# Seven half-size products for the scores of two tiles, and gathered rows added up on TensorE

## The chip, the cores and the metric

The kernel runs on one core of a Trainium2 chip. The metric is device time in microseconds (us); the time before is the median of three runs, 2519.51 us (2517.99 to 2520.62). Everything is fp32. A core has five engines with queues of their own[...]: PE (TensorE, matrix products, results in PSUM), DVE (VectorE), ACT (ScalarE), POOL (GpSimd, which here issues the gathers) and SP (which issues the other DMAs). PSUM is used here as three "pairs" of 2 x 512 columns and two single banks, `pv` and `pt`.

## The reference, cut to what matters

Four layers are added to an image batch x of 4 x 512 x 32 x 32; layers 0 to 2 are two attentions and a gate and are left as they are. Layer 3 reads a memory of 2048 rows of 512 numbers:

```python
q = jnp.transpose(x, (0, 2, 3, 1)).reshape(-1, C)      # 4096 tokens x 512, group-normalised
att = q @ mempool.T                                    # 4096 x 2048 scores
vals, idx = jax.lax.top_k(att, k)                      # k = 8
vals = jax.nn.softmax(vals, axis=1)
att_sparse = jnp.zeros_like(att).at[rows, idx].set(vals)
out = att_sparse @ mempool                             # 8 weighted rows per token
```

The result, turned back to channels first, is added to layer 3's input.

## The kernel before, in words

Layers 0 to 2 fill the first 2012 us or so; their matrix products already use seven half-size products in places (`seven`, L1048 for the sums). Layer 3 is the end. The memory, transposed, lies in SBUF as four tiles `memT[k]` of 128 channels x 2048 items (`load_memory`). Each image has 1024 tokens, 8 tiles of 128 (`tiles`, 32 in all). Per tile:

- `attention` (L1521): for each half of the items, 2 blocks of 512 items x 4 blocks of channels, so 16 matmuls of 128x128 by 128x512 per tile, 8 into each pair of banks; ScalarE copies each half to `att` (L1526).
- `pick`: VectorE's MAX8 (L1541) and FIND_INDEX8 (L1543) over 2048 scores; eight indirect DMAs on POOL (L1546) gather the eight rows to `got`; `tmx` (L1552) and the Exp on ScalarE (L1555) make the weights `et` and their sum `rs`; SP loads the tile's layer input `xr`.
- `read`: `weigh` (L1563, L1564) divides the weights by the sum; VectorE makes acc, the first row times its weight (L1591), and adds the other seven (L1593); four transposes on TensorE (L1598) turn acc back to channels first.
- `put`: VectorE adds `xr` (L1603) and SP stores the result (L1604).

The loop runs these on different tiles: at step s, scores of tile s, search of tile s-1, put of s-3, read of s-2. The order on each engine is written out by hand: an instruction passed through `pin` stays in the order of the code with the other pinned ones of its engine. The last two tiles (`read_last`, L1579) are read by another way: eight diagonal matrices of the weights (`diagonals`, L1570), and 32 matmuls that add up and turn back the eight rows in PSUM. `prepare3` loads and normalises the next image's tokens in four ScalarE steps (L1506). The first tile's scores are made ahead of the last projection of layer 2 (`put_out2`, L199, L1478), and that projection's results are layer 3's input for the fourth image.

Of the kernel before, what the change touches and what calls it, by code (L numbers as in the profile page):

```python
# [41 lines left out]
def fast_net(ctx: ExitStack, tc: tile.TileContext, a: dict, out: bass.AP, flag: bass.AP):  # L42
# [13 lines left out]
    def pin(ins):  # L56

        return tc.keep_in_program_order(ins)
# [131 lines left out]
    def tokens(src):  # L190
        return lambda k, n: src[:, k, n * NB:(n + 1) * NB]

    def project(w, rhs, m, at, evacuate, name="proj"):


        ps = place(at, f"{name}_{m}")
        for n in range(T // NB):
            for k in range(KC):
                pin(nc.tensor.matmul(  # L199
                    ps[:, n, :], w[:, k, m * P:(m + 1) * P], rhs(k, n),  # L200
                    start=(k == 0), stop=(k == KC - 1),
                ))
        evacuate(flat2(ps))
# [1259 lines left out]
        nc.vector.tensor_mul(  # L1463
            I["o"][:, m, n * NB:(n + 1) * NB], I.pop(("pv", m, n)), I.pop(("rb", m, n)))

    def put_out2(b):
        I = img[b]
        s1 = l2[b][1]
        mv = small.tile([P, KC, 2], F32, tag="mv", name=f"mv_d{b}")

        def add_out(m, ps):
            st = small.tile([P, 2, 6], F32, tag="bnst", name=f"st_d{b}_{m}")
            for n in range(T // NB):
                xr = apool.tile([P, NB], F32, tag="xr", bufs=2, name=f"xr_c{b}_{m}_{n}")
                nc.sync.dma_start(out=xr, in_=x1[b][:, m, n * NB:(n + 1) * NB])
                pin(nc.scalar.activation(
                    xr, xr, AF.Identity, bias=I["tb"][:, m:m + 1], scale=s1[:, m:m + 1]))
                nc.vector.tensor_add(xr, ps[:, n * NB:(n + 1) * NB], xr)  # L1478
                nc.sync.dma_start(out=x2[b][:, m, n * NB:(n + 1) * NB], in_=xr)
                nc.vector.bn_stats(st[:, n, :], xr)  # L1480
            nc.vector.bn_aggr(mv[:, m, :], st.rearrange("p i s -> p (i s)"))

        for m in range(KC):
            project(I["Wp"], tokens(I["o"]), m, None, lambda ps: add_out(m, ps), f"p2_{b}")
        gc3 = const.tile([P, 2, KC], F32, tag=f"gc3_{b}", name=f"gc3_{b}")
        l3[b] = (mv, gc3)

# [21 lines left out]
            ))  # L1509
            yield  # L1510

    def attention(b, tt, between=None):

        nm = f"{b}_{tt}"
        att = eight_k([P, NI], f"att_{nm}")
        for i, (lo, hi) in enumerate(
                ((0, T), (T, T + NB), (T + NB, NI)) if (b, tt) == tiles[-1] else ((0, T), (T, NI))):
            sc = flat2(next_pair())
            for i0 in range(lo, hi, NB):
                for k in range(KC):  # L1520
                    pin(nc.tensor.matmul(  # L1521
                        sc[:, i0 - lo:i0 - lo + NB],
                        xn3[b][:, k, tt * P:(tt + 1) * P], memT[k][:, i0:i0 + NB],
                        start=(k == 0), stop=(k == KC - 1),
                    ))
            pin(nc.scalar.copy(att[:, lo:hi], sc[:, 0:hi - lo]))  # L1526
            if between is not None and i == 0:
                between()
        return att

    def pick(b, tt, att):

        nm = f"{b}_{tt}"
        top = small.tile([P, TOPK], F32, tag="top", name=f"top_{nm}")
        if (b, tt) == tiles[-1]:
            tops = small.tile([P, 3, TOPK], F32, tag="tops", bufs=1, name="tops")
            for i, (lo, hi) in enumerate(((0, T), (T, T + NB), (T + NB, NI))):
                pin(nc.vector.max(tops[:, i, :], att[:, lo:hi]))
            pin(nc.vector.max(top, tops.rearrange("p i n -> p (i n)")))
        else:  # L1540
            pin(nc.vector.max(top, att))  # L1541
        ix = small.tile([P, TOPK], mybir.dt.uint32, tag="ix", name=f"ix_{nm}")
        pin(nc.vector.max_index(ix, top, att))  # L1543
        got = big("qkv"[(b * TC + tt) % 3], f"got_{nm}").rearrange("p k (i c) -> p (k i) c", c=C)
        for i in range(TOPK):
            pin(nc.gpsimd.indirect_dma_start(  # L1546
                out=got[:, i, :], out_offset=None, in_=a["mem"],
                in_offset=bass.IndirectOffsetOnAxis(ap=ix[:, i:i + 1], axis=0),
                bounds_check=NI - 1, oob_is_err=False,
            ))  # L1550
        nmx = small.tile([P, 1], F32, tag="nmx", name=f"tmx_{nm}")
        pin(nc.vector.tensor_scalar_mul(nmx, top[:, 0:1], -1.0))  # L1552
        et = small.tile([P, TOPK], F32, tag="et", name=f"et_{nm}")
        rs = small.tile([P, 1], F32, tag="rs", name=f"trs_{nm}")
        nc.scalar.activation(et, top, AF.Exp, bias=nmx, scale=1.0, accum_out=rs)  # L1555
        i = (b * TC + tt) % 3
        xr = eT_flat[:, i * NB:(i + 1) * NB].rearrange("p (k q) -> p k q", q=P)
        nc.sync.dma_start(out=xr, in_=x2[b][:, :, tt * P:(tt + 1) * P])
        return got, et, rs, xr

# [9 lines left out]
            pin(nc.scalar.activation(dg[:, i, :], ident, AF.Identity, scale=et[:, i:i + 1]))  # L1570
        return dg

    def read_last(b, tt, picked, dg):

        got, et, rs, xr = picked
        tp = next_bank().rearrange("p (k q) -> p k q", q=P)
        for i in range(TOPK):
            for m in range(KC):
                pin(nc.tensor.matmul(  # L1579
                    tp[:, m, :], got[:, i, m * P:(m + 1) * P], dg[:, i, :],  # L1580
                    start=(i == 0 and m == 0), stop=(i == TOPK - 1),
                    skip_group_check=True,
                ))
        return tp, xr

    def read(b, tt, picked):
        got, et, rs, xr = picked
        nm = f"{b}_{tt}"
        weigh(et, rs, nm)
        acc = apool.tile([P, NB], F32, tag="rb", bufs=2, name=f"acc_{nm}")  # L1590
        pin(nc.vector.tensor_scalar_mul(acc, got[:, 0, :], et[:, 0:1]))  # L1591
        for i in range(1, TOPK):
            pin(nc.vector.scalar_tensor_tensor(  # L1593
                acc, got[:, i, :], et[:, i:i + 1], acc, ALU.mult, ALU.add
            ))
        tp = next_bank().rearrange("p (k q) -> p k q", q=P)
        for m in range(KC):
            pin(nc.tensor.transpose(tp[:, m, :], acc[:, m * P:(m + 1) * P], ident))  # L1598
        return tp, xr

    def put(b, tt, done):
        tp, xr = done
        pin(nc.vector.tensor_add(xr, tp, xr))  # L1603
        nc.sync.dma_start(out=out_v[b, :, :, tt * P:(tt + 1) * P], in_=xr)  # L1604
# [244 lines left out]
        places7[key] = nine[3 * i:3 * i + 3]  # L1849
    places7["Wq"] = places7["Wp"]  # L1850
    nc.gpsimd.tensor_scalar_mul(same, same, 8.0 / T)
    tiles = [(b, tt) for b in range(B) for tt in range(TC)]
    atts, picks, sums = {}, {}, {}
    scores2(0, UNITS2[0])
    for b in range(B):
# [29 lines left out]
            first7[2]()  # L1885
        apply2(b, UNITS2[-1])
        if last:
            atts[0] = attention(*tiles[0], lambda: invert2(b))
            finish2(b)
            put_out2(b)  # L1890
            continue
        over_keys(b, *UNITS2[-1][:2])
        at_border[0] = True
# [39 lines left out]
    ahead, behind = iter(()), chain(behind, norm3(B - 1))  # L1933
    end = len(tiles)
    diags = {}

    def pick_last(s):
        at = s - 1
        picks[at] = pick(*tiles[at], atts.pop(at))
        put(*tiles[s - 3], sums.pop(s - 3))  # L1940
        weigh(*picks[at][1:3], f"{tiles[at][0]}_{tiles[at][1]}")

    for s in range(end + 3):
        closing = end - 1 <= s <= end
        if closing:
            pick_last(s)
        if s < end:
            b, tt = tiles[s]
            if s > 0:
                atts[s] = attention(b, tt, (lambda: diags.update(  # L1950
                    {0: diagonals(0, picks[end - 2][1])})) if closing else None)
        if 0 <= s - 1 < end and not closing:
            picks[s - 1] = pick(*tiles[s - 1], atts.pop(s - 1))
        if s == end:
            diags[1] = diagonals(1, picks[end - 1][1])
        if s >= 3 and not closing:
            put(*tiles[s - 3], sums.pop(s - 3))
        if 0 <= s - 2 < end:
            at = s - 2
            sums[at] = (read(*tiles[at], picks.pop(at)) if at < end - 2  # L1960
                        else read_last(*tiles[at], picks.pop(at), diags[at - end + 2]))
        if s < end and tt == 2:
            ahead = prepare3(b + 1) if b + 1 < B else iter(())
        if s < end and tt >= 2:
            next(ahead, None)
        if s < end and 1 <= s <= TC:
            next(behind, None)
        if s == TC + 2:
            check_range()
        if s == TC + 4:  # L1970
            again = nc.values_load(flag, min_val=0, max_val=1)
    return again


# [702 lines left out]
```

## Time and profile before

| | |
|---|---|
| median of three runs | 2519.51 us |
| the profiled execution | 2519.18 us, span 2517.5 us, mean granted TensorE clock 0.998 |
| busy, share of the span | PE 98%, DVE 72%, ACT 41%, POOL 49% |
| layer 3, from the second tile to the last score (2068.2 to 2493.5, 425.3 us) | PE 425.3, DVE 345.8, ACT 89.2, POOL 270.0 us busy |
| chain that ended last, share of the span | PE 87%, of which L1521 17%; DMA 4%; DVE 3%; ACT 2% |

Busy time of PE is modelled, so it is read together with the idle time and the chain. The chain of waits is followed back from the last instruction: where it stays on one engine that engine sets the pace. In a group, the number after the count is the busy total and then the mean of one; after the last bar stands the engine's idle time ahead of the group and what ended it. PE records are shown singly: a matmul here leaves two, a transpose one.

### The profile page before, as it was taken

The page shows a single profiled execution, that of the slowest core. Times are in us where ns is not written, and L with a number is a line of the kernel's source. Part 1 is how long each engine was busy: PE and PEld are TensorE (multiplying, and loading weights), DVE is VectorE, ACT ScalarE, POOL GpSimd, SP SyncE. Part 2 cuts the span into 40 slices and gives each one's busy share as a digit, 9 for nine tenths or more (in the row PEclk, how much of TensorE's full clock was granted, in tenths as well). Part 3 has the DMA queues.
Part 4 walks back from the last instruction along what each step waited for, and adds up shares of the span by engine and source line. Part 5 has one row for each costly group of instructions (what it writes and reads, how often), then busy time and mean ns, then how long its engine had stood idle before and what let it go on. Part 6 is the DMA issues. An engine that isn't in the chain of part 4 may idle for free.

```text
span 2517.5 us, 48084 instructions
## 1 busy us (share of the span) xinstructions
PE 2474.3 (98%) x18512; PEld 1174.9 (47%) x18512; DVE 1822.0 (72%) x2962; ACT 1022.8 (41%) x1245; POOL 1224.0 (49%) x1688
## 2 busy tenths in 40 slices
PE   9999999999999999999999999999999999999998
PEld 4344534555355534555633633453363344444445
DVE  5789568875788548886768677676757647887876
ACT  1567346652666336651253145225324512121212
POOL 3266526553465426554274247127405617566665
PEclk9999999999999999999999999999999999999999
DMA  2597448872698538893301230131114046667666
GB/s 85 156 233 218 118 128 228 239 218 84 176 241 233 137 89 218 241 244 122 109 25 52 108 130 18 63 110 46 55 46 138 24 138 189 214 190 220 182 189 178
DMA packets 190033, 367.20 MB, mean 146 GB/s; under 512 B 32986, under 2 KB 96474, under 8 KB 185571
## 3 DMA queue, kind: packets, MB, share of 16 engines
q1 hardware_dynamic: 109712, 186.58, 23.9%
q0 software_dynamic: 49152, 142.79, 20.6%
q10 hardware_dynamic: 30930, 34.66, 5.1%
q8 instruction: 149, 2.44, 0.4%
q14 instruction: 90, 0.73, 0.1%
HBM read 190.10 MB, written 39.58 MB: 91 GB/s over the span
## 4 chain that ended last, share of the span: by engine, by line
PE 87%; DMA 4%; DVE 3%; ACT 2%; issue 1%; POOL 1%; SPq 0%; ACTq 0%; POOLq 0%
PE pair L1521 17%; PE pair L1121 12%; PE pair L1369 8%; PE pv L578 8%; PE pair L513 6%; PE pair L199 6%; PE pair L539 6%; PE pt L471 5%; PE pt L1406 4%; PE pv L1406 4%; PE pair L1247 4%; PE pt L767 4%; DMA s<-ss 3%; ACT e L546 2%; DVE out L1048 1%
## 5 line engine op out<-in xcount | busy, mean ns | idle before, releaser
L528 POOL DMA_DIRECT2D s<-ss x512 | 258.1, 511 | 398.6 <-issue 115.0
L552 DVE STREAM_TRANSPOSE eT<-e 128x1024 f32<-128x1024 f32 x256 | 316.6, 1237 | 186.5 <-ACT e L546 186.1
L1546 POOL DMA_INDIRECT got<-in_mem,ix x256 | 279.3, 1091 | 213.2 <-DVE tmx L1552 144.4
L1363 ACT ACTIVATE eT<-pair 128x1024 f32<-128x1024 f32 x256 | 248.5, 1022 | 314.8 <-PE pair L1369 188.8
L567 DVE BATCH_NORM_STATS2 st<-e 128x6 f32<-128x256 f32 x1024 | 350.7, 404 | 0.0
L1387 POOL TENSOR_TENSOR e<-eT 128x1024 f32<-128x1024 f32 x96 | 239.0, 2493 | 171.7 <-ACT eT L1363 122.6
L546 ACT ACTIVATE e<-pair 128x1024 f32<-128x1024 f32 x256 | 250.4, 1022 | 165.8 <-PE pair L539 137.2
L519 ACT COPY ss<-pair 128x1024 f32<-128x1024 f32 x256 | 247.2, 1020 | 86.7 <-PE pair L513 42.7
L513 PE MATMUL pair<-k,q 64*32 64x512 f32 x4096 | 267.3, 598 | 12.7 <-ACT e L546 12.7
L578 PEld LDWEIGHTS pv<-eT,v 128*64 128x64 f32 x4096 | 221.1, 137 | 72.0 <-issue 55.2
L578 PE MATMUL pv<-eT,v 128*64 128x128 f32 x4096 | 250.0, 275 | 4.5 <-ACT pv L638 4.5
L1369 PE MATMUL pair<-q,k 64*128 64x512 f32 x1024 | 239.9, 605 | 1.8 <-DVE sum L1048 0.9
L1388 DVE TENSOR_TENSOR eT<-eT,e 128x1024 f32<-128x1024 f32 x96 | 142.5, 1485 | 132.5 <-POOL e L1387 132.3
L539 PE MATMUL pair<-s,wmix 32*32 32x512 f32 x4096 | 162.7, 599 | 3.4 <-DMA s<-ss 3.3
L1593 DVE SCALAR_TENSOR_TENSOR acc<-got,et,acc 128x512 f32<-128x512 f32 x210 | 157.9, 752 | 7.5
L1383 POOL TENSOR_TENSOR eT<-eT 128x1024 f32<-128x1024 f32 x32 | 82.4, 2576 | 161.5 <-ACT eT L1363 154.2
L1369 PEld LDWEIGHTS pair<-q,k 64*128 64x128 f32 x1024 | 92.3, 186 | 140.0 <-issue 66.6
L1526 ACT COPY att<-pair 128x1024 f32<-128x1024 f32 (+1 forms) x65 | 64.9, 999 | 217.2 <-PE pair L1521 217.1
L513 PEld LDWEIGHTS pair<-k,q 64*32 64x32 f32 x4096 | 57.0, 105 | 178.4 <-ACT e L546 86.7
L1048 DVE TENSOR_TENSOR k<-k,pair 128x512 f32<-128x512 f32 (+1 forms) x96 | 78.1, 857 | 65.8 <-PE pair L1121 52.1
L1541 DVE MAX8 top<-att 128x8 f32<-128x2048 f32 x31 | 71.1, 2293 | 71.3 <-ACT att L1526 71.3
L651 POOL TENSOR_TENSOR o<-pv,rb 64x256 f32<-64x256 f32 x128 | 118.8, 928 | 6.3
(383 smaller groups left out, 3752.7 us busy)
## 6 DMA issues: line engine op xcount, KB each, us to landing
s<-ss SPq DMA_DIRECT2D x512, 128.0 KB
s<-ss POOLq DMA_DIRECT2D x512, 128.0 KB, 4.6
rb<-r POOLq DMA_DIRECT2D x64, 128.0 KB, 6.0
o<-o SPq DMA_DIRECT2D x32, 256.0 KB
xr_c<-x SPq DMA_DIRECT2D x32, 256.0 KB
rb_c<-r SPq DMA_DIRECT2D x64, 128.0 KB
eT<-x SPq DMA_DIRECT2D x32, 256.0 KB
out<-eT SPq DMA_DIRECT2D x32, 256.0 KB
```

The costliest lines, as they stand in the source:

```text
L513: pin(nc.tensor.matmul(sc[m * NS:(m + 1) * NS, r, :], q[r * HD:(r + 1) * HD, m, s * NS:(s + 1) * NS], k_[r * HD:(r + 1) * HD, m, n * NB:(n ...
L528: pin(relays[side].dma_start(out=s2[2 * m + r::NH], in_=ss[m * NS:(m + 1) * NS, r, :]))
L539: pin(nc.tensor.matmul(mixed(s, r // 2)[t * NS:(t + 1) * NS, r % 2, :].rearrange("p (qq k) -> p qq k", qq=2), wmix[r * NS:(r + 1) * NS], s ...
L546: pin(nc.scalar.activation(e[:, half].rearrange("p r qq k -> p (r qq k)"), flat2(mixed(s, half)), AF.Exp))
L552: pin(nc.vector.transpose(eT[:, j % 2].rearrange("p b (qq i r) x -> p i r qq b x", qq=2, i=4)[:, i, 2 * half:2 * half + 2], e[:, half].rea ...
L567: pin(nc.vector.bn_stats(st[:, i, 2 * half + r, qq, :], e[:, half, r, qq, :]))
L578: pin(nc.tensor.matmul(pv[r * HD:(r + 1) * HD, gp, :], I["v"][:, t, g * HD:(g + 1) * HD], eT[:, j % 2, t, :, 4 * g:4 * g + 4], start=(t == ...
L1121: pin(nc.tensor.matmul(ps[:, m, :], w[:, k, m * P:(m + 1) * P], x[:, k, :], start=(k == 0), stop=(k == 1)))
L1363: pin(nc.scalar.activation(e, scs[len(es)], AF.Exp, scale=SCALE))
L1369: pin(nc.tensor.matmul(sc[:, r, :], I["k"][r * HD:(r + 1) * HD, m, t * P:(t + 1) * P], I["q"][r * HD:(r + 1) * HD, m, n * NB:(n + 1) * NB] ...
L1521: pin(nc.tensor.matmul(sc[:, i0 - lo:i0 - lo + NB], xn3[b][:, k, tt * P:(tt + 1) * P], memT[k][:, i0:i0 + NB], start=(k == 0), stop=(k == ...
L1546: pin(nc.gpsimd.indirect_dma_start(out=got[:, i, :], out_offset=None, in_=a["mem"], in_offset=bass.IndirectOffsetOnAxis(ap=ix[:, i:i + 1], ...
```

## The change

Two tiles of one image, tt+4 and tt, are scored together. Their tokens' channels in two halves and the items' channels and items in two halves form a product of 2 x 2 by 2 x 2 blocks. It is made of seven products of half size in place of eight, with sums of token blocks (`token_sums`, and s4) and of memory blocks (`memory_sums`, made once on VectorE during `put_out2`). Five of the seven products add up without a break in two pairs of PSUM banks (x four times, z twice, so that ScalarE copies a partial sum and later products are added onto it in PSUM); y holds the seventh. Four results are copied by ScalarE and three added by VectorE. The first two and the last two tiles are scored as before.

In `read`, now `ready`, `add_up` and `turn_back`, the last gathered row (even tiles) or the last two (odd tiles) aren't added on VectorE: TensorE multiplies acc and those rows by diagonal matrices that ScalarE makes, and adds the results up in PSUM while turning them. ScalarE makes the first product of acc too, and the division by the sum of the weights is taken into the diagonals. `xr` and the diagonals lie in `e`, a buffer of layer 2, since the memory sums take the place of `xr`.

```diff
-tiles = [(b, tt) for b in range(B) for tt in range(TC)]
+tiles = [(b, t) for b in range(B) for tt in range(TC // 2) for t in (tt + 4, tt)]

+    def memory_sums():
+        def raw(h, i):
+            return [memT[2 * h + k][:, i * T:(i + 1) * T] for k in range(2)]
+        t1, t2, t3, t4 = ([t[:, k, :] for k in range(2)] for t in mem_t)
+        for out, x, y in ((t1, raw(0, 1), raw(0, 0)), (t2, raw(1, 1), t1),
+                          (t3, raw(1, 1), raw(0, 1)), (t4, raw(1, 0), t2)):
+            for part in zip(out, x, y):
+                sub7(*part)
+            yield
+    def token_sums(n):
+        a11, a12, a21, a22 = token_blocks(n)
+        s1, s2, s3, s4 = token_places
+        sub7(s3, a11, a21)
+        add7(s1, a21, a22)
+        sub7(s2, s1, a11)
+    def two_tiles(n):
...
+        x, z, y = (next_pair() for _ in range(3))
+        next_pair()
+        sub7(s4, a12, s2)
...
+        for ps, start, a_, b_, use, to in (
+                (x, True, a11, raw(0, 0), "=", one[:, left]),
+                (z, True, s3, of(2), "=", other[:, right]),
+                (x, False, s2, of(1), "=", other[:, left]),
+                (z, False, a22, of(3), "+", other[:, left]),
+                (x, False, s1, of(0), "+", other[:, right]),
+                (y, True, a12, raw(1, 0), "+", one[:, left]),
+                (x, False, s4, raw(1, 1), "=", one[:, right])):
+            for c in range(2):
+                for k in range(2):
+                    pin(nc.tensor.matmul(
+                        ps[:, c, :], a_[:, k, :], b_(k, c),
+                        start=(start and k == 0), stop=(k == 1), skip_group_check=True))
+            if use == "=":
+                pin(nc.scalar.copy(to, flat2(ps)))
+            elif ps is not y:
+                add7(to, to, flat2(ps))
+            yield other
+            if ps is y:
+                last = lambda: add7(one[:, left], one[:, left], flat2(y))
+        last()
+        yield one

-    def read(b, tt, picked):
-        weigh(et, rs, nm)
-        pin(nc.vector.tensor_scalar_mul(acc, got[:, 0, :], et[:, 0:1]))
-        for i in range(1, TOPK):
-            pin(nc.vector.scalar_tensor_tensor(
-                acc, got[:, i, :], et[:, i:i + 1], acc, ALU.mult, ALU.add
-        for m in range(KC):
-            pin(nc.tensor.transpose(tp[:, m, :], acc[:, m * P:(m + 1) * P], ident))
+    def weighed(n):
+        return TOPK - 1 - n % 2
+    def ready(n, picked):
+        pin(nc.vector.reciprocal(ri, rs))
+        pin(nc.scalar.activation(acc, got[:, 0, :], AF.Identity, scale=et[:, 0:1]))
+        diags = [spare[:, 3 * NB + i * P:3 * NB + (i + 1) * P] for i in range(3)]
+        pin(nc.scalar.activation(diags[0], ident, AF.Identity, scale=ri))
+        for i in range(weighed(n), TOPK):
+            dg = diags[1 + i - weighed(n)]
+            pin(nc.scalar.activation(dg, diags[0], AF.Identity, scale=et[:, i:i + 1]))
+        return acc, diags
+    def add_up(n, picked, acc):
+        for i in range(1, weighed(n)):
+            pin(nc.vector.scalar_tensor_tensor(
+                acc, got[:, i, :], et[:, i:i + 1], acc, ALU.mult, ALU.add
+    def turn_back(n, picked, made):
+        terms = [(acc, diags[0])] + [
+            (got[:, i, :], diags[1 + i - weighed(n)]) for i in range(weighed(n), TOPK)]
+        for i, (rows, dg) in enumerate(terms):
+            for m in range(KC):
+                pin(nc.tensor.matmul(
+                    tp[:, m, :], rows[:, m * P:(m + 1) * P], dg,
...
+    for n in range(2, end - 2, 2):
+        b, j = tiles[n][0], n // 2 % (TC // 2)
+        parts = two_tiles(n)
+        next(parts)
+        picks[n - 1] = pick(n - 1, atts.pop(n - 1))
+        if j == 1:
+            ahead = prepare3(b + 1) if b + 1 < B else iter(())
+        next(ahead, None)
+        next(parts)
+        if n > 2:
+            turn_to(n - 3)
+            put(n - 3, sums.pop(n - 3))
+        made[n - 2] = ready(n - 2, picks[n - 2])
+        add_up(n - 2, picks[n - 2], made[n - 2][0])
+        if j == 3:
+            next(ahead, None)
+        next(parts)
+        next(behind, None)
...
+        next(parts)
+        if j == 2:
+            next(ahead, None)
+        atts[n] = next(parts)
+        turn_to(n - 2)
+        made[n - 1] = ready(n - 1, picks[n - 1])
+        next(parts)
+        picks[n] = pick(n, atts.pop(n))
+        put(n - 2, sums.pop(n - 2))
+        next(parts)
+        atts[n + 1] = next(parts)
+        if n + 2 < end - 2:
+            token_sums(n + 2)
+        add_up(n - 1, picks[n - 1], made[n - 1][0])
```

`turn_to(n)` is `turn_back` of tile n. In the loop's two left-out lines the range flag is computed at n = 12 and loaded by the engines at n = 14, as before at two steps of the loop. In what follows P1 to P7 are the seven products in the order of the table in `two_tiles`, a pair is two tiles scored together, and the turn of a tile is its `turn_back`.

More of the change, by code (lines that the diff above doesn't have):

```diff
@@ L1464, in finish2, with put_out2 @@
             I["o"][:, m, n * NB:(n + 1) * NB], I.pop(("pv", m, n)), I.pop(("rb", m, n)))
-    def put_out2(b):
+    def put_out2(b, between):
         I = img[b]
@@ L1484, in put_out2 @@
             project(I["Wp"], tokens(I["o"]), m, None, lambda ps: add_out(m, ps), f"p2_{b}")
+            next(between)
         gc3 = const.tile([P, 2, KC], F32, tag=f"gc3_{b}", name=f"gc3_{b}")
@@ L1510, in prepare3, with new_att, attention @@
             yield
-    def attention(b, tt, between=None):
-        nm = f"{b}_{tt}"
-        att = eight_k([P, NI], f"att_{nm}")
+    spare = e.rearrange("p i r qq k -> p (i r qq k)")
+    att_at = [None]
+    def new_att(n, at=None):
+        return eight_k([P, NI], f"att_{n}", at)
+    def attention(n, between=None, at=None):
+        b, tt = tiles[n]
+        att = new_att(n, at)
         for i, (lo, hi) in enumerate(
-                ((0, T), (T, T + NB), (T + NB, NI)) if (b, tt) == tiles[-1] else ((0, T), (T, NI))):
+                ((0, T), (T, T + NB), (T + NB, NI)) if n == len(tiles) - 1 else ((0, T), (T, NI))):
             sc = flat2(next_pair())
@@ L1529, in attention @@
         return att
-    def pick(b, tt, att):
+    mem_t = [eT_flat[:, i * NI:(i + 1) * NI].rearrange("p (k q) -> p k q", k=2) for i in range(4)]
+    def memory_sums():
[7 more added lines that the diff above has]
+            yield
@@ new lines, in token_blocks, with raw, of @@
+    def token_blocks(n):
+        b, tt = tiles[n]
+        return [xn3[b][:, 2 * h:2 * h + 2, t * P:(t + 1) * P] for t in (tt - 4, tt) for h in range(2)]
+    def token_sums(n):
[5 more added lines that the diff above has]
+    def two_tiles(n):
+        a11, a12, a21, a22 = token_blocks(n)
+        s1, s2, s3, s4 = token_places
+        free = [at for at in range(3) if at != att_at[0]]
+        one, other = new_att(n + 1, free[0]), new_att(n, free[1])
+        att_at[0] = free[0]
+        x, z, y = (next_pair() for _ in range(3))
+        next_pair()
+        sub7(s4, a12, s2)
+        def raw(h, i):
+            return lambda k, c: memT[2 * h + k][:, i * T + c * NB:i * T + (c + 1) * NB]
+        def of(i):
+            return lambda k, c: mem_t[i][:, k, c * NB:(c + 1) * NB]
+        left, right = slice(0, T), slice(T, NI)
+        for ps, start, a_, b_, use, to in (
[20 more added lines that the diff above has]
+        yield one
@@ L1533, in pick @@
+    def pick(n, att):
+        b, tt = tiles[n]
         nm = f"{b}_{tt}"
         top = small.tile([P, TOPK], F32, tag="top", name=f"top_{nm}")
-        if (b, tt) == tiles[-1]:
+        if n == len(tiles) - 1:
             tops = small.tile([P, 3, TOPK], F32, tag="tops", bufs=1, name="tops")
@@ L1543, in pick @@
         pin(nc.vector.max_index(ix, top, att))
-        got = big("qkv"[(b * TC + tt) % 3], f"got_{nm}").rearrange("p k (i c) -> p (k i) c", c=C)
+        got = big("qkv"[n % 3], f"got_{nm}").rearrange("p k (i c) -> p (k i) c", c=C)
         for i in range(TOPK):
@@ L1554, in pick @@
         rs = small.tile([P, 1], F32, tag="rs", name=f"trs_{nm}")
-        nc.scalar.activation(et, top, AF.Exp, bias=nmx, scale=1.0, accum_out=rs)
-        i = (b * TC + tt) % 3
-        xr = eT_flat[:, i * NB:(i + 1) * NB].rearrange("p (k q) -> p k q", q=P)
+        pin(nc.scalar.activation(et, top, AF.Exp, bias=nmx, scale=1.0, accum_out=rs))
+        xr = spare[:, n % 3 * NB:(n % 3 + 1) * NB].rearrange("p (k q) -> p k q", q=P)
         nc.sync.dma_start(out=xr, in_=x2[b][:, :, tt * P:(tt + 1) * P])
@@ L1571, in diagonals, with read_last @@
         return dg
-    def read_last(b, tt, picked, dg):
+    def read_last(picked, dg):
         got, et, rs, xr = picked
@@ L1584, in read_last @@
         return tp, xr
-    def read(b, tt, picked):
+    def weighed(n):
+        return TOPK - 1 - n % 2
+    def ready(n, picked):
         got, et, rs, xr = picked
-        nm = f"{b}_{tt}"
-        weigh(et, rs, nm)
-        acc = apool.tile([P, NB], F32, tag="rb", bufs=2, name=f"acc_{nm}")
-        pin(nc.vector.tensor_scalar_mul(acc, got[:, 0, :], et[:, 0:1]))
-        for i in range(1, TOPK):
+        ri = small.tile([P, 1], F32, tag="ri", name=f"tri_{n}")
+        acc = apool.tile([P, NB], F32, tag="rb", bufs=2, name=f"acc_{n}")
+        pin(nc.vector.reciprocal(ri, rs))
[7 more added lines that the diff above has]
+    def add_up(n, picked, acc):
+        got, et, rs, xr = picked
+        for i in range(1, weighed(n)):
             pin(nc.vector.scalar_tensor_tensor(
@@ L1595, in read, with put @@
             ))
+    def turn_back(n, picked, made):
+        got, et, rs, xr = picked
+        acc, diags = made
         tp = next_bank().rearrange("p (k q) -> p k q", q=P)
-        for m in range(KC):
-            pin(nc.tensor.transpose(tp[:, m, :], acc[:, m * P:(m + 1) * P], ident))
-        return tp, xr
-    def put(b, tt, done):
+        terms = [(acc, diags[0])] + [
[4 more added lines that the diff above has]
+                    tp[:, m, :], rows[:, m * P:(m + 1) * P], dg,
+                    start=(i == 0 and m == 0), stop=(i == len(terms) - 1),
+                    skip_group_check=True,
+                ))
+        return tp, xr
+    def read(n, picked):
+        made = ready(n, picked)
+        add_up(n, picked, made[0])
+        return turn_back(n, picked, made)
+    def put(n, done):
+        b, tt = tiles[n]
         tp, xr = done
@@ L1887, in fast_net @@
         if last:
-            atts[0] = attention(*tiles[0], lambda: invert2(b))
+            atts[0] = attention(0, lambda: invert2(b))
             finish2(b)
-            put_out2(b)
+            put_out2(b, memory_sums())
             continue
@@ L1931, in check_range, with turn_to @@
             flag, tps[0:1, 0:1], float(2 * P * NS * B * (TC + 2 * KC)), None, ALU.not_equal)
-    ahead, behind = iter(()), chain(behind, norm3(B - 1))
+    behind = chain(behind, norm3(B - 1))
+    at_border[0] = True
     end = len(tiles)
     diags = {}
+    both = [apool.tile([P, 2, 2, P], F32, tag="xr", bufs=2, name=f"tokens_{i}") for i in range(2)]
+    token_places = [t[:, i] for t in both for i in range(2)]
+    atts[1] = attention(1)
+    picks[0] = pick(0, atts.pop(0))
+    token_sums(2)
+    att_at[0] = (turns8[0] - 1) % 3
+    made = {}
+    def turn_to(n):
+        sums[n] = turn_back(n, picks.pop(n), made.pop(n))
+    ahead = iter(())
+    for n in range(2, end - 2, 2):
[16 more added lines that the diff above has]
+        next(behind, None)
+        if n == 12:
+            check_range()
+        if n == 14:
+            again = nc.values_load(flag, min_val=0, max_val=1)
+        next(parts)
[12 more added lines that the diff above has]
+        add_up(n - 1, picks[n - 1], made[n - 1][0])
     def pick_last(s):
         at = s - 1
-        picks[at] = pick(*tiles[at], atts.pop(at))
-        put(*tiles[s - 3], sums.pop(s - 3))
+        picks[at] = pick(at, atts.pop(at))
+        put(s - 3, sums.pop(s - 3))
         weigh(*picks[at][1:3], f"{tiles[at][0]}_{tiles[at][1]}")
-    for s in range(end + 3):
+    for s in range(end - 2, end + 3):
         closing = end - 1 <= s <= end
@@ L1946, in fast_net @@
             pick_last(s)
[L1947 to L1953, printed above, removed]
+        if s == end - 2:
+            atts[s] = attention(s, lambda: turn_to(s - 3), (att_at[0] + 1) % 3)
+        if s == end - 1:
+            atts[s] = attention(s, lambda: diags.update(
+                {0: diagonals(0, picks[end - 2][1])}), (att_at[0] + 2) % 3)
+        if s - 1 < end and not closing:
+            picks[s - 1] = pick(s - 1, atts.pop(s - 1))
         if s == end:
             diags[1] = diagonals(1, picks[end - 1][1])
-        if s >= 3 and not closing:
-            put(*tiles[s - 3], sums.pop(s - 3))
-        if 0 <= s - 2 < end:
+        if not closing:
+            put(s - 3, sums.pop(s - 3))
+        if s - 2 < end:
             at = s - 2
[L1960 to L1971, printed above, removed]
+            sums[at] = (read(at, picks.pop(at)) if at < end - 2
+                        else read_last(picks.pop(at), diags[at - end + 2]))
     return again
```

## The prediction

> **What bounds the kernel now.** I read the page's busy row first, then the stage of layer 3 in the chain of waits, then the groups of that stage by shape, then one tile in the timeline.
>
> The page, busy us and share of the span:
>
> ```profile
> PE 2474.3 (98%) x18512; PEld 1174.9 (47%) x18512; DVE 1822.0 (72%) x2962; ACT 1022.8 (41%) x1245; POOL 1224.0 (49%) x1688
> ```
>
> The chain of waits over layer 3 (start us, us, what):
>
> ```profile
> 2082.16 0.44 PE pt L1598 x4
> 2082.60 13.73 PE pair L1521 x32
> 2096.33 0.44 PE pv L1598 x4
> ...
> 2493.61 0.44 PE pt L1598 x4
> 2494.05 7.16 PE pv L1579 x64
> 2501.23 0.52 DVE eT L1603
> 2501.75 4.97 DMA got<-in_mem,ix
> ```
>
> TensorE sets the end from 2012.6 to 2493.6 without a gap: a tile is 13.73 us of scores and 0.44 of transposes, 14.17 together. At 2501 the chain leaves TensorE: the last tile's gathered rows are awaited. Two more readings: a matmul is two records and a transpose one (16 matmuls make x32, four transposes x4), and 32 matmuls of 128 columns with gathered rows as stationary operand (L1579) take 7.16 us, 0.2237 each, against 0.11 for a transpose of the same shape.
>
> Groups of the whole trace by shape (count | busy us, mean ns | idle before):
>
> ```profile
> L1598 PE MATMUL pt<-ident,acc 128*128 128x128 f32 x64 | 9.6, 273 | 0.0
> L1526 ACT COPY att<-pair 128x1024 f32<-128x1024 f32 x63 | 63.8, 1012 | 214.3 <-PE pair L1521 214.2
> L1593 DVE SCALAR_TENSOR_TENSOR acc<-got,et,acc 128x512 f32<-128x512 f32 x210 | 157.9, 752 | 7.5
> L1048 DVE TENSOR_TENSOR q<-q,pair 128x1024 f32<-128x1024 f32 x24 | 28.7, 1218 | 16.4 <-PE pair L1121 11.4 <-ACT q L1257 5.0
> L1048 DVE TENSOR_TENSOR eT<-eT 128x256 f32<-128x256 f32 x20 | 7.1, 416 | 0.0
> ```
>
> Timeline, one tile on VectorE:
>
> ```profile
> 2452.17 2.29 DVE L1541 MAX8 top<-att 128x8 f32<-128x2048 f32 x1 [2.21 <-ACT att L1526]
> 2454.58 2.29 DVE L1543 FIND_INDEX8 ix<-top,att 128x8 uint32<-128x2048 f32 x1
> 2456.78 0.13 DVE L1552 TENSOR_SCALAR tmx<-top 128x1 f32<-128x1 f32 x1
> 2458.66 5.48 DVE L1593 SCALAR_TENSOR_TENSOR acc<-got,et,acc 128x512 f32<-128x512 f32 x7
> ```
>
> VectorE works 12.0 of the tile's 14.17 us and waits 2.2 for the next copy: the second engine, near the first.
>
> [...] a record here takes 0.429 (13.73/32) and 0.112 (7.16/64), so cost goes with records and columns. [...]
>
> **The change part by part.**
>
> *Scores, TensorE.* 28 of 32 tiles (14 pairs) go from 32 matmuls per pair to 28. One matmul is 13.73/16 = 0.858. 14 x 4 x 0.858 = **48.1 us removed**.
>
> *Turning back, TensorE.* Four transposes per tile become four matmuls for acc, and four more per weighed row: 8 for an even tile (one row), 12 for an odd one (two). By L1579: 1.79 and 2.68 us for 0.44. Up to the last score matmul tiles 0 to 28 are turned back: 15 even, 14 odd, 288 matmuls x 0.2237 = 64.4; removed 29 x 0.44 = 12.8. **51.6 us added.** The bounds of the unit price are 0.214 (a quarter of 0.858) and 0.2237: 48.9 to 51.6. I take the upper, the same operation.
>
> Tile 29's turn (+2.24) comes after the last score. Before, TensorE is done there at 2501.2 and starts on the last rows at 2502.4, then waits for each; its later start, about 1 us, is made up while rows land 1.3 us apart (their issue spacing). Cost nothing; without that cover 1.0.
>
> *VectorE.* Per pair it gains three 128x1024 sums (3 x 1.22) and four 128x256 token sums (4 x 0.42), +5.3; it loses three row additions (3 x 0.78), two first products (2 x 0.49) and two weight scalings (2 x 0.48 as spaced in that tile), -4.3. So 24 us become 25 of a pair that TensorE makes 24.03 + 1.79 + 2.68 = 28.5 long (28.34 before). VectorE is still not the bound; the order of its work decides whether TensorE waits.
>
> *The order, one pair, t = 0 at its first product.* A product is 4 x 0.858 = 3.43. TensorE: P1 0, P2 3.43, turn of tile n-3 6.86, P3 9.55, P4 12.98, P5 16.42, turn of n-2 19.85, P6 21.64, P7 25.07, end 28.5. An evacuation starts 0.2 after a product's last slot (2450.93 and 2451.13 in the timeline).
> VectorE: add of P5 20.05 to 21.3; reciprocal; max and index of tile n (4.67) to 26.1; put 0.68; add of P6 to 28.0; three token sums to 29.2; five row additions to 33.1, which is 4.6 of the next pair; s4 to 5.0; max and index of n-1 to 9.7; put, waiting for the turn at 9.75, to 10.4; reciprocal. Then it waits for acc from ScalarE.
> ScalarE: copy of P1 by 4.7; Exp of n-1 waits for VectorE until 9.8 and takes 0.5; **queued behind it** the copy of P2 (10.3 to 11.3), which P4 needs at 12.98: 1.7 spare. Then acc (0.81 by L1476; at least 0.585, a copy of that size) and two diagonals (0.39, 0.31) to 12.9; copy of P3 13.2 to 14.2, needed by P5 at 16.42.
> VectorE adds six rows 12.1 to 16.8 (turn of n-2 at 19.85: 3.0 spare), adds P4 to 18.0, and waits for P5 until 20.05. So the cycle closes with 2 us of slack on VectorE, the turn of n-3 has 2.2 and s3 2.7. **No wait in an ordinary pair.**
>
> *Normalisation of the next image, ScalarE.* Four 1.23 us operations, two in the third and two in the fourth pair of an image, for three images. One sits ahead of the copy of P2, which then ends at 12.6 against 12.98. In the fourth pair another sits ahead of the copy of P3: it ends at 16.5 to 17.0 against 16.42, a wait of 0.1 to 0.6; two such at 0.3 are **0.6**. The third of them (pair 14) also has the flag load, and there the listing of the changed program puts acc of tile n-1 ahead of that normalisation and of the copy of P3. It needs n-1's first row: gather issued at 10.0, landing 3.9 to 4.6 later (the median of the gathers, and 2497.85 to 2502.43 in the timeline), 14.2; then 0.81 + 0.31 + 1.23 + 1.02 end at 17.7, so P5 waits **1.3**.
>
> *Memory sums.* Eight 1.22 us operations, two after each of the four projections, a projection being 6.9 us of which VectorE uses 2.8: 5.2 of 6.9. Tile 0's search moves 2.4 us later, its token sums to 2068.2, ahead of P2 at 2071.6. Nothing; without that cover 2.4 once.
>
> *DMA and queues.* As many gathers, loads and stores as before. Three input loads move ahead of tile 0's normalisation rows on SP's queue: about 0.9 us on a rescaling whose result TensorE first reads 11 us later. The gathers of the two tiles are issued 16.4 and 12.1 us apart and a tile's eight take 11.0 of POOL: hidden with 1.1 to spare.
>
> *Sum.* -48.1 + 51.6 + 0.6 + 1.3 = +5.4. The span of 2517.5 becomes 2522.9; the profiled execution's 2519.18, 1.7 around its span, becomes 2524.6. The median of the runs, 2519.51, is 0.3 above that: 2524.9.
>
> **Rivals.**
> *A, no waits at all:* ScalarE's pieces are shorter than taken, or the spares larger. For it: the waits are tenths of a microsecond worked out of gaps. Then only the matmul balance stays, +0.8 to +3.5: 2520.3 to 2523.0, not slower beyond what can be told.
> *B, the copy of P2 is late in every pair:* the Exp ahead of it waits for a VectorE chain of 18 us. For it: 1.7 us is a tenth of that chain, and VectorE is 88% busy. Against: my spacings include the gaps of the timeline. It decides once that Exp starts later than about 11.5 us after P1; each microsecond beyond costs 14. At one, 2539; at half, 2532.
> *C, a matmul by a diagonal is as cheap as a transpose:* 288 x 0.11 = 31.7 in place of 64.4, giving 2492. Against: L1579's x64 records for 32 matmuls. It would also be the case of a turn that hides behind other work, but TensorE has no gap in that stage.
>
> **How the numbers follow.** Medians here tell about 0.2%, 5 us, from no change. My case 0.46: it spans +4 to +7, a third of it below 5. A 0.23, B 0.25, C 0.06. So faster 0.06, same 0.23 + 0.15 = 0.38, slower 0.31 + 0.25 = 0.56. The range runs from inside A, 2521, to B at about six tenths of a microsecond, 2534; C and the end of B, 0.15 or so, lie outside. My case's own range is 2523.5 to 2526.5.
>
> **What would show it.** Right: the products at 0.858 a matmul, 392 of them; 300 matmuls of 128 columns at 0.22; 28.5 us from one pair to the next; VectorE near 25 in it; in the chain TensorE alone except in the fourth pairs. Wrong: idle of TensorE ahead of P4 in most pairs, put down to ScalarE's copy (B); pairs near 26 us (C); waits for rows or token sums; a row-by-diagonal price that differs amid scores from that of a run of its own.

## The result, and the profile after

The changed kernel takes 2538.75 us (median of six runs, 2535.80 to 2541.06), the kernel before 2519.36 beside it (2517.44 to 2521.07): a ratio of 1.0081, 95% interval 1.0071 to 1.0091, or 19.4 us slower. The forecast was 2524.9 with a range to 2534.0: the direction was right, the size was not. The profiled execution of the changed kernel is the 2535.80 one, with a span of 2534.1 against 2517.5.

The page's busy row and the group of the row additions of the changed kernel (count | busy us, mean ns | idle before, releaser):

```profile
PE 2481.4 (98%) x18880; PEld 1211.0 (48%) x18880; DVE 1839.1 (73%) x2963; ACT 1066.7 (42%) x1350; POOL 1221.4 (48%) x1688
...
L1683 DVE SCALAR_TENSOR_TENSOR acc<-got,et,acc 128x512 f32<-128x512 f32 x165 | 124.0, 751 | 44.4 <-ACT acc L1672 39.7
```

TensorE is still at 98%. The row additions are 45 fewer, as the change says, but 39.7 us of VectorE's idle time now stand ahead of them, ended by ScalarE's first product (L1672).

The chain of waits of the changed kernel through the first pairs (start us, us, what):

```profile
2063.51 10.30 PE pair L1594 x24
2073.81 0.12 PE pt L152 x2
2073.93 6.97 PE pair L1594 x16
2080.90 1.78 PE pt L1695 x16
2082.68 13.73 PE pair L1594 x32
2096.42 2.68 PE pv L1695 x24
2099.10 10.30 PE pair L1594 x24
2109.40 1.78 PE pt L1695 x16
```

This is the ordinary pair of the forecast: 10.30 + 1.78 + 13.73 + 2.68, 28.5 us from one to the next, TensorE without a gap. A product and a turn cost just what the sum says.

The waits of the changed kernel that are new and whose chain reaches TensorE in layer 3 (engine, what, line, for what: us in total, times, longest):

```profile
DVE acc L1683 <- ACT acc L1672: 39.7, 16, 13.4
...
PE pv L1695 <- DVE acc L1683: 6.8, 1, 6.8
...
PE pt L1695 <- DVE acc L1683: 5.3, 1, 5.3
...
PE pair L1594 <- ACT att L1598: 1.6, 1, 1.6
```

Three waits of TensorE, each once. Two of them are for acc of a single tile. The timeline of the changed kernel shows where, in the last 70 us (start us, us, engine, line, operation; in brackets the idle time before it and what ended it):

```profile
2478.77 1.01 ACT L1534 COPY att<-pair 128x1024 f32<-128x1024 f32 x1 [8.54 <-PE pair L1529]
2479.97 0.71 ACT L1672 ACTIVATE acc<-got,et 128x512 f32<-128x512 f32 x1
2480.72 4.70 DVE L1683 SCALAR_TENSOR_TENSOR acc<-got,et,acc 128x512 f32<-128x512 f32 x6 [8.05 <-ACT acc L1672]
2485.56 2.04 PE L1695 MATMUL pv<-e,acc 128*128 128x128 f32 x8 [6.83 <-DVE acc L1683]
2487.40 1.91 PE L1695 MATMUL pv<-e,got 128*128 128x128 f32 x8
...
2503.19 0.59 ACT L1534 COPY att<-pair 128x512 f32<-128x512 f32 x1 [2.85 <-PE pair L1529]
2503.67 0.72 ACT L1672 ACTIVATE acc<-got,et 128x512 f32<-128x512 f32 x1
2504.43 3.90 DVE L1683 SCALAR_TENSOR_TENSOR acc<-got,et,acc 128x512 f32<-128x512 f32 x5 [13.36 <-ACT acc L1672]
2508.24 2.41 DVE L1615 MAX8 tops<-att 128x8 f32<-128x1024 f32 x3
2508.47 2.04 PE L1695 MATMUL pt<-e,acc 128*128 128x128 f32 x8 [5.32 <-DVE acc L1683]
```

Both times the same thing happens. `ready` of tile 28 is called after the scores of tile 30, so the first product stands behind both score copies of that tile on ScalarE. The gather of the tile's first row was issued at 2460.51 (3.5 to 4.8 us from issue to landing in that stretch) and VectorE began the reciprocal, called just ahead of the product, at 2472.51, but the copies began at 2469.22 and 2478.77, and the product only behind them. ScalarE is idle for 8.54 us before the second copy, because it waits for TensorE to finish the scores; acc is made at 2479.97, VectorE, idle for 8.05, then adds six rows, and TensorE, out of scores, waits 6.83 for the sum. For tile 29 the wait of VectorE is 13.36, and behind its five additions stands the search of tile 31, the last link to the end. In the kernel before, VectorE made tile 29's first product itself (L1591) and had no such queue to stand in. Its lines in the timeline of the kernel before, with the search of tile 31 (L1538):

```profile
2486.57 0.49 DVE L1591 TENSOR_SCALAR acc<-got,et 128x512 f32<-128x512 f32 x1
...
2492.48 2.48 DVE L1538 MAX8 tops<-att 128x8 f32<-128x1024 f32 x3
```

After the wait TensorE is slow: 16 records of a turn take 3.75 us (2485.56 to 2489.31 in the chain) where an ordinary turn takes 1.78; for tile 29, 24 records take 5.05 (2508.47 to 2513.52) in place of 2.68. By the windows of this trace TensorE's granted clock, the share of full speed that it was given, was 0.50 over those 3.75 us and 0.52 over the 5.05, behind waits of 6.83 and 5.32; it was 1.00 over the 3.59 us (2250.47 to 2254.06) behind the wait of 1.55 below. In the seven products alone, below, matmuls were slower after waits of 2.22 us already.

The third wait is in the pair of tiles 14 and 15, in the timeline of the changed kernel:

```profile
2247.37 0.72 ACT L1672 ACTIVATE acc<-got,et 128x512 f32<-128x512 f32 x1 [2.46 <-DMA got<-in_mem,ix]
...
2249.42 0.99 ACT L1598 COPY att<-pair 128x1024 f32<-128x1024 f32 x1
2250.47 3.70 PE L1594 MATMUL pair<-eT,tokens 128*128 128x512 f32 x8 [1.55 <-ACT att L1598]
```

**Where 16.6 us went, profile against profile** (2534.1 - 2517.5). Layers 0 to 2 ended earlier in this execution, by 4.7: the first pair starts at 2063.51, the kernel before starts its third tile, the first to be compared with that pair, at 2068.20 (this is the start of the stage in the table of the profile before, which calls it the second tile). Their matrix products are unchanged, and executions of the kernel before alone spread from 2514 to 2526. From there to the last score: 439.7 against 425.4, +14.3, of which the balance of matmuls is 3.5, pair 14 1.6, the wait for tile 28 6.8 and the half-speed turn behind it 2.0, together 13.9. After the last score: 30.9 against 23.9, +7.0, of which 6.2 is the late search of tile 31. It starts at 2508.24, 5.1 after the last score; before, at 2492.48, 1.1 ahead of it.

### The profile page after: what moved, and what is told of

It is laid out like the page before. It is cut to its first block, busy times and chain, and to the rows that moved or that the text cites. A ratio compares the mean times of both kernels' runs of the same rounds, so it can differ in the third digit from the quotient of the medians.

```text
span 2534.1 us, 49009 instructions
## 1 busy us (share of the span) xinstructions
PE 2481.4 (98%) x18880; PEld 1211.0 (48%) x18880; DVE 1839.1 (73%) x2963; ACT 1066.7 (42%) x1350; POOL 1221.4 (48%) x1688
## 4 chain that ended last, share of the span: by engine, by line
PE 86%; DVE 6%; DMA 3%; ACT 3%; issue 2%; POOL 1%; SPq 0%; POOLq 0%; ACTq 0%; DVEq 0%
PE pair L1594 12%; PE pair L1121 12%; PE pair L1369 8%; PE pv L578 8%; PE pair L513 6%; PE pair L199 6%; PE pair L539 5%; PE pt L471 5%; PE pt L1406 4%; PE pv L1406 4%; PE pair L1247 4%; PE pt L767 4%; PE pair L1529 2%; ACT e L546 2%; DMA s<-ss 2%
## 5 line engine op out<-in xcount | busy, mean ns | idle before, releaser
L1594 PE MATMUL pair<-eT,tokens 128*128 128x512 f32 x448 | 201.3, 592 | 1.6 <-ACT att L1598 1.6
L1683 DVE SCALAR_TENSOR_TENSOR acc<-got,et,acc 128x512 f32<-128x512 f32 x165 | 124.0, 751 | 44.4 <-ACT acc L1672 39.7
L1594 PEld LDWEIGHTS pair<-eT,tokens 128*128 128x128 f32 x448 | 84.0, 190 | 102.8 <-issue 99.5
L1048 DVE TENSOR_TENSOR k<-k,pair 128x512 f32<-128x512 f32 (+1 forms) x96 | 78.1, 857 | 65.9 <-PE pair L1121 52.2
```

What stands on the lines that cost most here:

```text
L1594: pin(nc.tensor.matmul(ps[:, c, :], a_[:, k, :], b_(k, c), start=(start and k == 0), stop=(k == 1), skip_group_check=True))
```

## The experiments

All of them compute the whole function. The kernel before, run beside them, has medians of 2520.31 (10 runs, beside the tail, the flag, the seven products alone and the cheaper turn) and 2519.3 (19 runs, beside the other three); each ratio is against it.

### The tail's order

`ready` of the last ordinary tiles goes between the halves of the scores, so that ScalarE makes acc while TensorE still works on scores.

```diff
...
-            atts[s] = attention(s, lambda: turn_to(s - 3), (att_at[0] + 1) % 3)
+            atts[s] = attention(s, lambda: (turn_to(s - 3), made.update(
+                {s - 2: ready(s - 2, picks[s - 2])})), (att_at[0] + 1) % 3)
-            atts[s] = attention(s, lambda: diags.update(
-                {0: diagonals(0, picks[end - 2][1])}), (att_at[0] + 2) % 3)
+            atts[s] = attention(s, lambda: (
+                made.update({s - 2: ready(s - 2, picks[s - 2])}),
+                diags.update({0: diagonals(0, picks[end - 2][1])})), (att_at[0] + 2) % 3)
```

> The changed kernel with one move: for tiles 28 and 29 the ScalarE products for acc and the diagonals, and the reciprocal ahead of them, stand between the score copies of tiles 30 and 31 and not behind all of them. Same instructions, same matmuls. Theory I (the loss beyond the matmul balance is the order of ScalarE's queue in the last tiles: 6.8 us of wait ahead of the turn of tile 28 and 2.0 us of slower matmuls after it, 6.1 us of later search for tile 31 and 1.0 us of slower matmuls at the end): 15.9 us less than the changed kernel, so 2523, within 2521 to 2526, and 0.15% above the kernel before. Rival II (the last tiles are late because of the added matmuls, sums and gathers themselves, whatever the order): 2535 to 2541, as the changed kernel.

Measured: 2525.64 us (seven runs), ratio 1.0023 (1.0010 to 1.0037). Of TensorE's waits, these are left in layer 3 (view of the waits, this kernel):

```profile
PE pair L1594 <- ACT att L1598: 1.8, 1, 1.8
...
PE pt L1655 <- DMA got<-in_mem,ix: 1.5, 2, 0.7
```

Both waits for acc are gone, and 13 of the 19 us with them (2538.75 - 2525.64). What stays, 5.3 over the kernel before (2.5 to 9.3 by the interval), is what the forecast's sum had, 5.4. So the tail's order is the cause of the miss: it gives back 13.1 of the 13.9 by which the measured time was over the forecast.

### The flag load two tiles later

The load of a flag into registers, at which the order of ScalarE's work in pair 14 differs from the other pairs, is moved to the next pair, which has no normalisation.

```diff
-        if n == 14:
+        if n == 16:
```

> The changed kernel with the load of the range flag one pair later (n = 16, the first pair of an image, in place of n = 14). Theory I (the load lets the compiler order put acc of the next tile ahead of ScalarE's copy of P3, where it waits for its gathered row): TensorE's idle of 1.55 us ahead of P5 in pair 14 is gone, and no pair has more than 0.2. Rival II (the normalisations of the next image delay that copy, flag or not): pair 14 keeps 0.3 to 1.6 us, as do pairs 6 and 22. The total moves by no more than the runs scatter.

Measured: one run, 2533.47, span 2531.7 against 2534.1. Pair 14 is 28.5 long in place of 30.3 and the wait for ScalarE's copy is gone from the view of the waits, in which the two of the tail stand as they were:

```profile
PE pv L1695 <- DVE acc L1683: 6.8, 1, 6.8
PE pt L1695 <- DVE acc L1683: 5.3, 1, 5.3
```

The one wait that the forecast placed and sized in the middle of the stage is where the forecast said, and it goes with the flag load. One run can't tell its size from the scatter; the trace can.

### The seven products alone

The rows are weighed, added on VectorE and turned back by four transposes, as before the change (in this kernel and the next L1672 adds the rows and L1681 transposes).

```diff
     def ready(n, picked):
+        weigh(et, rs, f"n{n}")
-        pin(nc.scalar.activation(acc, got[:, 0, :], AF.Identity, scale=et[:, 0:1]))
...
     def add_up(n, picked, acc):
-        for i in range(1, weighed(n)):
+        pin(nc.vector.tensor_scalar_mul(acc, got[:, 0, :], et[:, 0:1]))
+        for i in range(1, TOPK):
...
     def turn_back(n, picked, made):
+        for m in range(KC):
+            pin(nc.tensor.transpose(tp[:, m, :], acc[:, m * P:(m + 1) * P], ident))
...
```

> The seven products alone: all eight rows are added on VectorE, weights are scaled there and acc is turned by four transposes, as in the kernel before, at the places of the changed kernel. Theory I (VectorE is then the bound: per pair three sums 3.7, token sums 1.7, two searches 9.3, two puts 1.4, two scalings 1.2, two first products and fourteen row additions 12.0, about 29 us against 24.9 of TensorE): pairs of 29 us or a little more, TensorE idle 4 us in each, no ScalarE waits in the last tiles, total 2526 to 2540. Rival II (the 48 us of removed matmuls arrive, since VectorE's share is hidden): pairs near 25 us, total near 2472.

Measured: 2550.71 us (four runs), ratio 1.0126 (1.0109 to 1.0143), slower than anything expected; a pair takes 30.2 to 31.4. TensorE alone would need 24.03 + 0.88. The waits of TensorE in this kernel:

```profile
PE pair L1594 <- ACT att L1598: 35.5, 13, 3.4
...
PE pv L1681 <- DVE acc L1672: 8.8, 6, 4.1
PE pt L1681 <- DVE acc L1672: 7.4, 8, 0.9
```

VectorE isn't full either. One stretch of 30 us of this kernel: its length, then the busy time (and count) of TensorE, its weight loads, VectorE, ScalarE and POOL, then TensorE's granted clock, the DMA share and GB/s:

```profile
2260.00:2290.00 30.00, 27.05 (x64) 11.90 (x64) 26.47 (x35) 5.56 (x9) 16.46 (x16) 0.94 0.72 210
```

Two engines, each waiting for the other: a ring. Its links stand in the timeline of this kernel:

```profile
2226.96 0.13 DVE L1629 TENSOR_SCALAR tmx<-top 128x1 f32<-128x1 f32 x1
...
2227.13 0.30 ACT L1632 ACTIVATE et<-top,tmx 128x8 f32<-128x8 f32 x1 [8.21 <-DVE tmx L1629]
...
2228.56 1.90 ACT L1598 COPY att<-pair 128x1024 f32<-128x1024 f32 x2
...
2229.60 5.40 PE L1594 MATMUL pair<-eT 128*128 128x512 f32 x8 [3.35 <-ACT att L1598]
...
2235.11 1.22 DVE L1048 TENSOR_TENSOR att<-att,pair 128x1024 f32<-128x1024 f32 x1 [1.58 <-PE pair L1594]
```

The Exp of tile n-1 waits 8.21 for VectorE's search; behind it in ScalarE's queue stands the copy of the second product; the fourth product may not be added onto that PSUM pair until it is copied; and VectorE, held up by its own waits for the fourth and fifth products, comes late to the next search. This is the mechanism of rival B, which the changed kernel escapes. It takes three row additions, two first products and two weight scalings per pair off VectorE, and its longer turn ahead of the third product (2.68 in place of 0.44) gives the copy more time as well; no run here separates the two. (In this pair a normalisation of 1.23 stands between the Exp and the copy too. It is in six of the fourteen pairs, and there the wait is 3.2 to 3.4; in the seven other pairs that wait it is 2.22.)

TensorE also pays in speed. After each of the thirteen waits eight records take 5.2 to 5.4 in place of 3.60, after the short ones too, and the clock over the stretch is 0.94:

```profile
2168.02 5.40 PE L1594 MATMUL pair<-eT 128*128 128x512 f32 x8 [2.22 <-ACT att L1598]
```

### The seven products alone, with the copy ahead of the Exp

The same kernel, in which `pick(n - 1)` comes after the second product: on ScalarE the copy then no longer stands behind the Exp, nor, in the six pairs that have one, behind the normalisation.

```diff
         next(parts)
+        next(parts)
         picks[n - 1] = pick(n - 1, atts.pop(n - 1))
...
-        next(parts)
         if n > 2:
```

> The seven products alone, as in the run of that name, with one move: the search of tile n-1, and with it its Exp, stands behind P2 in the code, so that ScalarE copies P2 before it waits for that Exp. Theory I (that run's pairs of 30.2 to 31.4 us are a ring: add of P5, VectorE's searches, sums and rows, Exp, copy of P2, P4, P5): the ring is cut, VectorE's own work is left, pairs of 28.5 to 29.3 us, total 2518 to 2532. Rival II (VectorE's amount of work alone made those pairs): pairs stay at 30 us or more, total 2546 to 2554.

Measured: 2518.17 us (twelve runs), ratio 0.9994 (0.9985 to 1.0004); pairs of 28.0 to 28.2 in the main, somewhat shorter than expected. The waits of TensorE, and the same stretch, of this kernel:

```profile
PE pv L1681 <- DVE acc L1672: 20.7, 13, 4.1
PE pt L1681 <- DVE acc L1672: 14.2, 11, 1.6
...
PE pair L1594 <- ACT att L1598: 3.3, 4, 1.0
```

```profile
2260.00:2290.00 30.00, 28.24 (x72) 12.61 (x71) 29.29 (x41) 5.69 (x10) 18.92 (x18) 1.00 0.67 202
```

The order of one copy and one Exp is worth some 32 us (2550.71 against 2518.17), so the ring was the cause; the normalisation moved as well, but the 2.22 us waits of the pairs without one are gone too. What bounds now is VectorE, 29.29 of 30 busy. The seven products save 48 us of TensorE and nothing of the whole, since VectorE has no room for the sums that they need. Some rows must go to TensorE; the changed kernel sends three of sixteen, at a high price.

### A cheaper turn

acc is transposed as before, and the one weighed row of each tile is added onto it by a diagonal in the same PSUM bank; ScalarE takes the division into the weights, so no acc has to be multiplied by a diagonal. The two changes above are in it too.

```diff
     def weighed(n):
-        return TOPK - 1 - n % 2
+        return TOPK - 1
...
+        pin(nc.scalar.activation(et, et, AF.Identity, scale=ri))
...
+        for m in range(KC):
+            pin(nc.tensor.transpose(tp[:, m, :], acc[:, m * P:(m + 1) * P], ident))
+            for i in range(weighed(n), TOPK):
...
+                    tp[:, m, :], got[:, i, m * P:(m + 1) * P], diags[i - weighed(n)],
+                    start=False, stop=(i == TOPK - 1), skip_group_check=True,
```

> The changed kernel with the moves of the last tiles and of the flag load, and with another turn: four transposes of acc and, added onto each in PSUM, a product with one gathered row only (weights scaled by ScalarE ahead of it). TensorE per pair 24.03 + 2 x (0.44 + 0.89) = 26.7, VectorE 25.0 + one more row addition 0.8 = 26 to 26.5. Theory I (TensorE's matmul balance sets a pair, and ScalarE's order the rest): pairs of 26.7 to 27.3 us against 28.34 before, total 2498 to 2506. Rival II (with VectorE within half a microsecond of TensorE its chain of searches and sums becomes the bound): pairs of 28 us or more, total 2515 or more.

Measured: 2509.25 us (four runs), ratio 0.9957 (0.9941 to 0.9974): a gain, but 3 above the expected range. A turn in the timeline of this kernel (L1691 the transpose, L1693 the matmul):

```profile
2308.70 0.27 PE L1691 MATMUL pv<-ident,acc 128*128 128x128 f32 x1
2308.81 0.39 PE L1693 MATMUL pv<-e,got 128*128 128x128 f32 x2
2309.03 0.27 PE L1691 MATMUL pv<-ident,acc 128*128 128x128 f32 x1
```

0.33 from one transpose to the next, 1.33 per tile, against 1.78 and 2.68. But six of the fourteen pairs take 28.1 where the others take 27.0 (0.3 more than TensorE's sum of 26.7), those with the next image's normalisation, and TensorE waits six times for ScalarE's copy, 6.7 in all:

```profile
2327.67 1.23 ACT L1507 ACTIVATE eT<-eT,gc 128x1024 f32<-128x1024 f32 x1
2328.80 0.99 ACT L1598 COPY att<-pair 128x1024 f32<-128x1024 f32 x1
...
2329.85 3.70 PE L1594 MATMUL pair<-eT,xn_d 128*128 128x512 f32 x8 [1.16 <-ACT att L1598]
```

The normalisation stands ahead of the copy of the second product. In the changed kernel the turn ahead of the third product was 1.35 longer (2.68 against 1.33), and there this normalisation cost no wait.

### The cheaper turn with ScalarE's order worked out anew

`ready` comes right after the first product, `pick` of n-1 after the second, and the normalisations stand behind the copies that TensorE waits for. The diagonals of the even and the odd tile now lie in two places. The cut is against the run above.

```diff
-        diags = [spare[:, 3 * NB + i * P:3 * NB + (i + 1) * P] for i in range(3)]
+        diags = [spare[:, 3 * NB + n % 2 * P:3 * NB + (n % 2 + 1) * P]]
...
         next(parts)
+        made[n - 2] = ready(n - 2, picks[n - 2])
+        next(parts)
         picks[n - 1] = pick(n - 1, atts.pop(n - 1))
...
         if j == 1:
             ahead = prepare3(b + 1) if b + 1 < B else iter(())
-        next(ahead, None)
-        next(parts)
+            next(ahead, None)
...
-        made[n - 2] = ready(n - 2, picks[n - 2])
...
-        if j == 3:
-            next(ahead, None)
...
-        if j == 2:
-            next(ahead, None)
+        if j >= 2:
+            next(ahead, None)
+            next(ahead, None)
```

> The version with transposes and one gathered row per tile on TensorE, reordered: P2's copy ahead of the Exp of tile n-1, acc and diagonal of tile n-2 made on ScalarE right after P1's copy (so that VectorE doesn't wait for them), and the four normalisations of the next image behind the copy of P3 in the third and fourth pair. Same instructions. Theory I (that version's pairs of 27.0 and 28.1 us are the ring through Exp and the normalisations ahead of the copy of P2): TensorE alone sets a pair, 26.7 us in all of them, total 2496 to 2502. Rival II (VectorE's total of work, or the gathers, is the bound by now): pairs of 27 us or more, total 2504 to 2510.

Measured: 2499.07 us (six runs), ratio 0.9914 (0.9901 to 0.9928), as expected. Every pair is 26.7 long, but for 26.9 where a small matmul of another kind stands between; of TensorE's waits in layer 3 only those for gathered rows in the closing products are left:

```profile
PE pt L1655 <- DMA got<-in_mem,ix: 3.6, 4, 1.4
```

### Half as many rows on TensorE

As the last, with a weighed row in the odd tiles alone.

```diff
     def weighed(n):
-        return TOPK - 1
+        return TOPK - n % 2
```

> As the reordered version, with a gathered row on TensorE only for odd tiles and eight rows on VectorE for even ones: TensorE 25.8 us per pair, VectorE 26.5. Theory I (VectorE becomes the bound, and TensorE, waiting in each pair, runs some matmuls slower): pairs of 26.5 to 27.5, total 2496 to 2510, no better than the version with one row per tile. Rival II (VectorE still has room): pairs near 25.8, total 2486 to 2493.

Measured: 2486.96 us (four runs), ratio 0.9867 (0.9851 to 0.9884): 32 us faster than the kernel before and 52 faster than the changed one (2538.75 - 2486.96). The same stretch, and the waits of TensorE in layer 3, of this kernel:

```profile
2260.00:2290.00 30.00, 30.00 (x83) 13.99 (x83) 29.20 (x38) 8.46 (x16) 19.59 (x19) 1.00 0.71 206
```

```profile
PE pt L1655 <- DMA got<-in_mem,ix: 2.8, 4, 1.0
...
PE pv L1691 <- DVE acc L1682: 0.7, 1, 0.7
```

A pair is 25.8 long, TensorE's own count: 24.03 + 0.44 + 1.33. VectorE is 97% busy and makes TensorE wait once, 0.7. The theory that VectorE would become the bound fell: its work was estimated at 26.5 a pair, and 29.20 of 30 us is 25.1 of a pair of 25.8.

## Why the prediction was wrong

**The step that failed** is the placing of waits: "Tile 29's turn (+2.24) comes after the last score ... Cost nothing", and with it "The order, one pair", which was worked out for an ordinary pair and taken to hold to the end. The cover named for tile 29's turn was that of a TensorE queue that starts 1 us late. But what the turn needs, acc, had been moved to ScalarE, and in the last steps, which follow another loop, ScalarE's queue has the score copies ahead of it. Tile 28's turn, counted at its plain length, waits for the same reason. The 6.8 of that wait, the 2.0 of half-speed matmuls behind it and the 6.2 of the late search were not in the sum, 15.0 together; mending the order of the tail gave back 13.1.

**Right, and shown**: the price of a matmul by a diagonal (1.78 and 2.68 for 8 and 12), of the products (0.858 a matmul), the balance of both (28.5 a pair), VectorE's load (25.4 of 30 us, or 24.1 of a pair, where 25 were forecast), no wait in an ordinary pair, and with the tail repaired a total of +5.3 against +5.4. That these two are so near is in part luck: the small waits in the sum came out otherwise, as told below, and the interval of the measured one is 2.5 to 9.3. The partial sums read in the middle of a group cost the copy or the addition alone, which in the forecast was its author's estimate: the copies of the pairs (L1598), three of four of them of a partial sum, took 1.006 us in the mean, those of whole groups (L1534) 1.012; the additions (L1048), one of three of a partial sum, took 1.216, and 1.218 for q in the layers before. Six products go into two PSUM pairs (four into x, two into z), four of the six are read with more to come, and TensorE still goes through a pair of tiles without a gap.

**Small errors.** Pair 14's wait is 1.55 against 1.3, by the mechanism given. The normalisation waits of 0.1 to 0.6 in the other fourth pairs did not come: the pairs of tiles 6 and 22 take 28.5, as an ordinary one.

**The rivals.** A (no waits) is right for the stage's pairs, except pair 14, and wrong for the whole. B, the late copy, didn't happen in the changed kernel, so that its figure for a wait of one microsecond, 2539, meets the measured 2538.75 by chance; but its ring is real: 35.5 us of waits in the seven products alone. C falls: the matmul costs twice the transpose (0.22 us against 0.11); its number, 2492, lies between two runs that turn by transposes (2499 and 2487), but these also send fewer rows to TensorE. The range held no case for a wait for acc outside the pairs; that, and not a price, made it too short.

## What to carry to other kernels

When a step is moved to another engine, walk that engine's queue through the loop's special ends as well as through its steady cycle: here the moved step stood behind two score copies in the last tiles, where the loop runs another order, and TensorE waited 6.83 us. Where two engines wait for each other and neither is full, look for a ring through a third one's queue before moving work; here the order of two instructions was worth some 32 us. Balance the split between engines by counted busy time, one row at a time: the best of the splits tried here loads the second engine to 97%.

## What was not expected of the hardware

- After an idle time of 6.83 us, TensorE's next 16 records took 3.75 us in place of 1.78, at a granted clock of 0.50. In the seven products alone waits of 2.22 to 3.35 did it too: each of the thirteen was followed by eight records in 5.2 to 5.4 us in place of 3.60, so a wait of 2.22 cost 1.8 more than itself. After 1.55 there was no such cost beyond 0.1.
- In the cheaper turn a transpose and the matmul that adds up onto it in the same PSUM bank took 0.11 and 0.22 us from start to start, as each in a run of its own (0.11 and 0.2237 in the profile before).
- VectorE busy for 29.20 of 30 us, with half as many rows on TensorE, left TensorE without one wait in that stretch (30.00 of 30 us busy).
